# Moving the first norms and transposes of a transformer's last part between the last output tiles of its attention

## Chip, cores and metric

The kernel runs on one core of one Trainium2 chip. The metric is device time in microseconds (us) of one execution. Before the change three runs took 1278.79, 1281.23 and 1281.28 us, a median of 1281.23.

## What is computed

Input is x, 4 batches of 512 rows with 512 features, and a context of the same shape. Four parts follow one another, each adding to x through a gate:

```python
x = x + tanh(g_xattn[0]) * L0_xattn(layernorm(x), ctx)         # one quantized product
x = x + tanh(g_ffn[0])   * L0_ffn(layernorm(x), w1, w2)        # two quantized products, GELU
x = x + tanh(g_xattn[1]) * L1_xattn(layernorm(x), ctx, ctx)    # 16 heads, 4 key groups, alibi, Wo
x = x + tanh(g_ffn[1])   * L1_ffn(layernorm(x))                # 2 of 8 experts, plus a shared MLP

# the last part, on the 2048 normalized rows
logits = xn @ router_w.T                                       # softmax, best 2, weights that sum to 1
moe    = sum over the chosen experts of  c_e * ((silu(xn @ gate_e) * (xn @ up_e)) @ down_e)
shared = (silu(xn @ s_gate + b) * (xn @ s_up + b)) @ s_down + b
```

The change lies at the border between the third part (attention) and the last.

## The kernel before

**Tiles.** Rows are held in 16 tiles of 128 (`x_sb[:, t, :]`, t = 0 to 15, four to a batch). x stays on the chip throughout. Everything is float32 except where the parts quantize. A float32 product of 128 x 512 shows as two passes in the profile, a transpose as one.

**Who orders the work.** The program is written in one sequence; a list scheduler then reorders it engine by engine, each instruction being issued when its inputs and memory are free, and the one written earlier going first. Two helpers restrain it. `tc.keep_in_program_order(ins)` ties an instruction behind the one that was written just before it on the same engine, and `tc.issue_after(ins)` ties a block behind a given instruction. Attention's products all go through `product` (line 237), which ties them, so TensorE's order in attention is the order written.

**Memory.** Tiles come from pools that lie as a stack from two ends of the on-chip memory. A pool that takes the place of closed ones can be written only when the readers of those are done.

**Attention's end.** The attention loop (lines 1095 to 1100) runs scores, softmax, weighted values and output products of different head groups interleaved. Its pools `qk` (queries and keys), `npool` and `one` (lines 1014 to 1016) are on the right side, `epool` (exponentials, partial sums, weighted values, line 1059) on the left; all four are closed together when the block of line 1058 ends. Behind the loop stand the last weighted values (`weigh`), two output products, `sums` of the last head group, and then the loop of lines 1105 to 1108. That loop does for each of the last four row tiles (12 to 15): `divide` (line 409: a reciprocal on VectorE, tied; a multiplication on GpSimd, line 414) and `given` (line 460), which is four output products of `project` (line 437) and the addition to x on VectorE (line 452). The sums depend on a chain of additions on GpSimd (`add_up`, line 389).

**The last part's start.** Behind attention come the pools `dpool` and `fpool` (lines 1116, 1117). `vx` (line 1119) holds the normalized rows with a row index and a weight beside each; 16 index fills on GpSimd write its index column (line 1121). Then come the load of the shared bias `sdb`, which is asked for on SyncE's queue (line 1126), and the loads of the shared weights (`load_shared`, line 1147). `normed(b)` (line 1160) takes the statistics of a batch (`layer_norm_stats`, line 115) and gives back four steps. Each normalizes one row tile on VectorE (`layer_norm`, line 129, instruction L130), transposes it in four pieces on TensorE into PSUM (L1170) and copies it to `xnT` on ScalarE (L1173). The steps of batch 0 run by themselves (lines 1296, 1297), those of the following batches between the gate and up products of the batch before (`shared_hidden`, line 1212, products L1219). The PSUM pool `big` has three buffers, which the transposes and the gate and up products share. Behind all batches come routing, the sorting of rows by expert through `slots` in device memory, the second half of the shared MLP and 36 tiles of expert rows, whose results are added to the output by indirect DMA (L1499).

Of the kernel before, what the change touches and what calls it, by code (L numbers as in the profile page):

```python
# [10 lines left out]
F32 = mybir.dt.float32  # L11
BF16 = mybir.dt.bfloat16
I32 = mybir.dt.int32
# [7 lines left out]
P = 128  # L21
B, S, D = 4, 512, 512
NT = B * S // P
TB = S // P
DC = D // P
# [10 lines left out]
RW = D + 2  # L36
# [12 lines left out]
def flamingo_kernel(  # L49
# [29 lines left out]
    def big(name):  # L79
        return ps_big.tile([P, 2, 512], F32, tag="big", name=name)  # L80
# [34 lines left out]
    def layer_norm_stats(b, tag, add=nc.vector):  # L115

        t0 = b * TB
        mv = small.tile([P, TB, 2], F32, tag="mv", name=f"mv_{tag}_{t0}")
        for i in range(TB):
            st = small.tile([P, 6], F32, tag="st", name=f"st_{tag}_{t0 + i}")  # L120
            nc.vector.bn_stats(st, x_sb[:, t0 + i, :])
            nc.vector.bn_aggr(mv[:, i, :], st)
        ve = small.tile([P, TB], F32, tag="ve", name=f"ve_{tag}_{t0}")
        add.tensor_scalar_add(ve, mv[:, :, 1], LN_EPS)
        rstd = small.tile([P, TB], F32, tag="rstd", name=f"rstd_{tag}_{t0}")
        nc.gpsimd.tensor_tensor(rstd, ve, mhalf, ALU.pow)
        return mv, rstd

    def layer_norm(dst, t, i, mv, rstd):
        nc.vector.tensor_scalar(  # L130
            dst, x_sb[:, t, :], mv[:, i, 0:1], rstd[:, i : i + 1], ALU.subtract, ALU.mult
        )
# [261 lines left out]
    def sums(b, g):  # L394
        parts = state.pop(("sum", b, g))
        sm = acc(f"sm_{b}_{g}")
        for k, part in enumerate(parts):
            for i in range(HPG):
                product(
                    sm[32 * i : 32 * i + 32, :],  # L400
                    lhsT=ones[:, :DH],
                    rhs=part[:, i, :],
                    start=k == 0,
                    stop=k == len(parts) - 1,
                )
        state["rec", b, g] = epool.tile([P, S], F32, tag="rec", name=f"rec_{b}_{g}", bufs=2)
        nc.scalar.copy(state["rec", b, g], sm)
# [647 lines left out]
            turn_units(1, 3)  # L1055


    with attention as ph:
        epool = ph.enter_context(tc.tile_pool(name="epool", bufs=3))
        wo_sb = place(2, "wo")[:, : DC * D].rearrange("p (c n) -> p c n", c=DC)  # L1060
        nc.sync.dma_start(out=wo_sb, in_=wo.rearrange("(c p) n -> p c n", p=P))


        rt_sb = const.tile([P, DC, 32], F32, name="rt_sb")
        nc.gpsimd.memset(rt_sb, 0.0)
        nc.sync.dma_start(out=rt_sb[:, :, :E], in_=routerT.rearrange("(c p) e -> p c e", p=P))
        sgb = const.tile([P, 2, 3], F32, name="sgb")
        sub = const.tile([P, 2, 3], F32, name="sub")
        nc.sync.dma_start(out=sgb, in_=s_gate_b)
        nc.sync.dma_start(out=sub, in_=s_up_b)  # L1070

        dram = ctx.enter_context(tc.tile_pool(name="dram", bufs=1, space=bass.MemoryType.DRAM))
        slots = dram.tile([MT * P, RW], F32, name="slots")
        empty = row_tables[:, 3 * NG * S + B * P :][:, : 2 * RW].bitcast(F32)
        nc.gpsimd.memset(empty, 0.0)
        nc.gpsimd.iota(
            empty[:, D : D + 1].bitcast(I32), [[0, 1]], base=B * S, channel_multiplier=1
        )

        def clear_slots(j0, j1):  # L1080
            if j0 < j1:
                nc.sync.dma_start(
                    out=slots[j0 * P : j1 * P, :].rearrange("(j p) d -> p j d", p=P),
                    in_=empty.unsqueeze(1).to_broadcast([P, j1 - j0, RW]),
                )


        before = const.tile([P, P], BF16, name="before")
        nc.gpsimd.memset(before, 1.0)
        nc.gpsimd.affine_select(  # L1090
            before, before, [[1, P]], ALU.is_gt, 0.0, base=0, channel_multiplier=-1
        )
        ones_h = const.tile([P, P], BF16, name="ones_h")
        nc.gpsimd.memset(ones_h, 1.0)
        for n in range(2, last_n + 3):
            for u in range(TB):
                turn_units(n, u)
            if n <= last_n:
                with tc.issue_after(state["fetch"]):
                    clear_slots(min(3 * (n - 2), MT), min(3 * (n - 2) + 3, MT))  # L1100
        weigh(*state["pend"])
        o3[2]()
        o3[3]()
        sums(*groups[-1])
        for i in range(TB):
            divide(*groups[-1], i)
            for f in given(NT - TB + i):
                f()

# [1 line left out]

    dpool = ctx.enter_context(tc.tile_pool(name="dpool", bufs=1))
    fpool = ctx.enter_context(tc.tile_pool(name="fpool", bufs=2))

    vx = dpool.tile([P, NT, RW], F32, name="vx")
    for t in range(NT):  # L1120
        nc.gpsimd.iota(
            vx[:, t, D : D + 1].bitcast(I32), [[0, 1]], base=t * P, channel_multiplier=1
        )
    places = [place(k, f"w_{k}") for k in range(3)]
    sdb = dpool.tile([P, D], F32, name="sdb")
    nc.sync.dma_start(out=sdb, in_=s_down_b.partition_broadcast(P))
# [27 lines left out]

    shared_w = [load_shared(n) for n in range(2)]

    xnT = dpool.tile([P, DC, NT * P], F32, name="xnT_d")
    prob = dpool.tile([P, NT, E], F32, name="prob")

    def normed(b):  # L1160

        state["d"] = layer_norm_stats(b, "d", nc.gpsimd)

        def one_tile(i):
            t = b * TB + i
            v = vx[:, t, :D]
            layer_norm(v, t, i, *state["d"])
            tp = big(f"tpd_{t}")
            for dc in range(DC):
                nc.tensor.transpose(  # L1170
                    tp[:, 0, dc * P : (dc + 1) * P], v[:, dc * P : (dc + 1) * P], ident
                )
            nc.scalar.copy(  # L1173
                xnT[:, :, t * P : (t + 1) * P], tp[:, 0, :].rearrange("p (c q) -> p c q", q=P)
            )

        return [lambda i=i: one_tile(i) for i in range(TB)]

    def routed():

        lgT = acc("lgT")
        for dc in range(DC):
            for b in range(B):
                nc.tensor.matmul(
                    lgT[32 * b : 32 * b + 32, :],
                    lhsT=rt_sb[:, dc, :],
                    rhs=xnT[:, dc, b * S : (b + 1) * S],
                    start=dc == 0,
                    stop=dc == DC - 1,
                )  # L1190
        strips = fpool.tile([P, S], F32, tag="row", name="strips", bufs=5)
        nc.scalar.copy(strips, lgT)
        tp = acc("tpr")
        for i in range(TB):
            nc.tensor.transpose(
                tp[:, i * P : (i + 1) * P], strips[:, i * P : (i + 1) * P], ident
            )
        nc.vector.tensor_copy(
            prob.rearrange("p (b i) e -> p b i e", b=B),
            tp.rearrange("p (i b e) -> p b i e", i=TB, b=B)[:, :, :, :E],  # L1200
        )
# [10 lines left out]
    def shared_hidden(n, b, h, chunks, between=()):  # L1212
        gw, uw, _ = shared_w[n]
        between = list(between)
        for c in range(chunks):
            gu = big(f"gu_{n}_{b}_{c}")
            for m, w in enumerate((gw, uw)):
                for dc in range(DC):
                    nc.tensor.matmul(  # L1219
                        gu[:, m, :],  # L1220
                        lhsT=w[:, dc, c * P : (c + 1) * P],
                        rhs=xnT[:, dc, b * S : (b + 1) * S],
                        start=dc == 0,
                        stop=dc == DC - 1,
                    )
            gate_up(gu, n, c, h[:, c, :], f"{n}_{b}_{c}")
            while between and (c == chunks - 1 or len(between) >= TB - c):
                between.pop(0)()

    def shared_halves(b, h):  # L1230

        gw, uw, _ = shared_w[1]
        gu = big(f"gu_h_{b}")
        for m, w in enumerate((gw, uw)):
            for dc in range(DC):
                for k in range(2):
                    nc.tensor.matmul(
                        gu[64 * k : 64 * k + 64, m, :],
                        lhsT=w[:, dc, 2 * P :],
                        rhs=xnT[:, dc, (b + k) * S : (b + k + 1) * S],  # L1240
                        start=dc == 0,
                        stop=dc == DC - 1,
                    )
        gate_up(gu, 1, 2, h, f"h_{b}")
# [48 lines left out]
                nc.sync.dma_start(out=out_t[:, t, :], in_=x_sb[:, t, :])  # L1293


    for f in normed(0):
        f()
    pend = None
    for b in range(B):
        h = hidden_rows(f"hd_0_{b}")  # L1300
# [312 lines left out]
```

## Time and profile before

| what | value |
| --- | --- |
| runs | 1278.79, 1281.23, 1281.28 us; median 1281.23 |
| the profiled execution | 1278.66 us, of which 1277.0 us span from its first to its last instruction |
| busy: TensorE | 1169.5 us, 92% of the span |
| busy: VectorE, ScalarE, GpSimd | 607.1 (48%), 510.9 (40%), 410.9 us (32%) |
| mean granted TensorE clock | 0.968 of full speed |
| read from and written to device memory | 113.84 and 32.32 MB |
| last attention score product ends | 684.83 us |
| last four output tiles on TensorE | from 692.07 us |
| first gate and up product | 710.68 us |
| router products | from 805.67 us |
| expert tiles | from about 957 us on |

All starts are counted from the beginning of the span. In lines of the profile PE is TensorE, PEld its weight loads, DVE VectorE, ACT ScalarE, POOL GpSimd and SPq the DMA queue of SyncE. A line of a timeline has start, length, engine, line of the code, operation, what it writes and reads, the shape and the number of instructions merged into it; in brackets stands how long the engine was idle before it and what ended that. `oc` are attention's output products, `tpd` the transposes of the last part's first norms, `gu` its gate and up products, `sm` attention's sums, `part` the partial sums. The busy time of TensorE contains waiting within its pipeline, so it is an upper bound.

### The profile page before, as it was taken

What the parts mean: (1) busy time and instruction counts of PE and PEld (TensorE: products, weight loads), DVE (VectorE), ACT (ScalarE), POOL (GpSimd) and SP (SyncE); (2) the same over time, 40 slices, a digit from 0 to 9 for tenths busy, and PEclk for the clock granted to TensorE, in tenths of its full rate; (3) what the DMA queues carried; (4) which work ended last, traced back from release to release, by engine and by line L of the source; (5) the groups of instructions that cost most, each with busy time, mean ns of one, the idle gap of its engine ahead of it and who ended that gap; (6) DMA issues with size and microseconds to landing.
All of it is one profiled execution on the core that took longest, in us unless ns stands there. A gap on an engine that the chain in (4) does not pass through costs nothing. (4 is left out here: it accounts for less than half of the span.)

```text
span 1277.0 us, 14308 instructions
## 1 busy us (share of the span) xinstructions
PE 1169.5 (92%) x5246; PEld 531.7 (42%) x5262; DVE 607.1 (48%) x1157; ACT 510.9 (40%) x710; POOL 410.9 (32%) x409
## 2 busy tenths in 40 slices
PE   3777897899899999999999999998999999999995
PEld 1333443344233333333333444443335555555553
DVE  7699999788557666656554511321221111111110
ACT  4688898686355554544454211100001112121121
POOL 1000100111277777767776311155000111111111
PEclk8878899999899999999999999998999999999998
DMA  9230232335021211211003000066116786888782
GB/s 342 72 131 12 42 62 42 85 79 118 28 68 34 67 35 35 67 34 59 2 1 141 9 1 1 0 230 183 62 63 189 231 266 187 262 262 253 202 247 34
DMA packets 88752, 135.32 MB, mean 106 GB/s; under 512 B 52836, under 2 KB 54120, under 8 KB 84840
## 3 DMA queue, kind: packets, MB, share of 16 engines
q1 hardware_dynamic: 80936, 116.52, 28.9%
q0 software_dynamic: 7744, 17.86, 6.6%
q8 instruction: 42, 0.69, 0.2%
q14 instruction: 30, 0.25, 0.1%
HBM read 113.84 MB, written 32.32 MB: 114 GB/s over the span
## 5 line engine op out<-in xcount | busy, mean ns | idle before, releaser
L428 ACT ACTIVATE ex<-s,mbias,mk 128x1024 f32<-128x1024 f32 x128 | 147.2, 1200 | 143.3 <-PE s L239 143.3
L319 DVE TENSOR_REDUCE nmax<-s 128x2 f32<-128x1024 f32 x128 | 150.3, 1215 | 100.4 <-PE s L239 89.6
L1463 PE MATMUL gue<-w,xT 128*128 128x352 f32 x576 | 176.1, 459 | 0.0
L1499 POOL DMA_INDIRECT out_dram<-ye,row_i x36 | 55.5, 1541 | 327.5 <-ACT ye L1498 230.1
L389 POOL TENSOR_TENSOR part<-part,ex 128x1024 f32<-128x1024 f32 x62 | 144.6, 2352 | 16.5 <-PE sm L239 11.4
L1219 PE MATMUL gu<-xnT_d,w 128*128 128x512 f32 x320 | 140.4, 593 | 0.7 <-ACT xnT_d L1173 0.7
L1463 PEld LDWEIGHTS gue<-w,xT 128*128 128x128 f32 x576 | 109.2, 190 | 70.6 <-issue 16.9
L1483 DVE COPY hT<-tph_e 128x256 f32<-128x256 f32 x36 | 15.3, 425 | 255.2 <-PE tph_e L1481 255.2
L1490 PE MATMUL oe<-w,hT 128*128 128x512 f32 (+1 forms) x216 | 102.4, 609 | 3.8 <-ACT ye L1498 0.6
L1219 PEld LDWEIGHTS gu<-xnT_d,w 128*128 128x128 f32 x320 | 59.9, 190 | 73.9 <-issue 72.1
L761 PE MATMUL oa<-ctx,vTa 128*128 128x512 f32 x128 | 69.5, 694 | 18.8 <-ACT vTa L758 18.7
L1207 ACT ACTIVATE sg<-gu,sgb 128x512 f32<-128x512 f32 x20 | 13.7, 687 | 175.9 <-PE gu L1219 154.0
L389 POOL TENSOR_TENSOR part<-ex,ex 128x1024 f32<-128x1024 f32 x32 | 75.8, 2388 | 24.1 <-ACT ex L428 24.1
L1471 ACT ACTIVATE sge<-gue 128x352 f32<-128x352 f32 x36 | 16.8, 465 | 151.5 <-PE gue L1463 151.5
L239 PE MATMUL s<-row_tables 10*128 10x512 bf16 (+1 forms) x512 | 67.7, 387 | 9.3 <-DVE nmax L319 5.9
L239 PE MATMUL s<-k,qT 32*128 32x512 f32 x512 | 72.8, 610 | 0.4 <-ACT qT L287 0.4
L239 PE MATMUL s<-qT,k 32*128 32x512 f32 x512 | 71.8, 601 | 0.0
L239 PE MATMUL av<-ex,kv 128*32 128x512 f32 x512 | 70.1, 612 | 0.4 <-ACT ex L428 0.4
L239 PE MATMUL q_ps<-xnT,wq_sb 128*128 128x512 f32 (+1 forms) x156 | 69.4, 557 | 0.0
L912 PE MATMUL ob<-w2q,hqT 128*128 128x512 bf16 x248 | 58.8, 381 | 11.3 <-DVE hqT L838 10.4
L1208 DVE SCALAR_TENSOR_TENSOR hd<-gu,sub,sg 128x512 f32<-128x512 f32 x20 | 15.0, 750 | 111.7 <-ACT sg L1207 98.8
L239 PE MATMUL oc<-wo,attnT 128*128 128x512 f32 (+1 forms) x164 | 66.2, 525 | 0.0
(261 smaller groups left out, 1648.6 us busy)
## 6 DMA issues: line engine op xcount, KB each, us to landing
w<-in_e_w_dram SPq DMA_DIRECT2D x36, 1408.0 KB
w<-in_e_w_dram SPq DMA_DIRECT2D x36, 768.0 KB
slots<-row_tables SPq DMA_DIRECT2D x13, 771.0 KB
xr<-slots SPq DMA_DIRECT2D x36, 256.0 KB
stage<-in_w1T_dram SPq DMA_DIRECT2D x4, 1024.0 KB
stage<-in_w2T_dram SPq DMA_DIRECT2D x4, 1024.0 KB
k<-kv SPq DMA_DIRECT2D x64, 64.0 KB
out_dram<-x_sb SPq DMA_DIRECT2D x16, 256.0 KB
```

The lines of the kernel that those rows point to most:

```text
L239: tc.keep_in_program_order(nc.tensor.matmul(*args, **how))
L319: largest = nc.vector.tensor_reduce(nmax[:, i, 2 * j : 2 * j + 2], sc[j], AX.X, ALU.max, negate=True)
L389: nc.gpsimd.tensor_tensor(part[:, hs, :], old[:, hs, :], ex[:, hs, :], ALU.add)
L428: nc.scalar.activation(ex[:, 2 * j : 2 * j + 2, :], sc[j], AF.Exp, bias=mbias[:, b, kc : kc + 1], scale=mk[:, b, kc : kc + 1],)
L761: nc.tensor.matmul(o_ps[:, 0, :], lhsT=vT[:, dc, :], rhs=cq[:, dc, :], start=dc == 0, stop=dc == DC - 1,)
L912: nc.tensor.matmul(o_ps, lhsT=hqT[:, c, :], rhs=w2q[:, c * D : (c + 1) * D], start=c == 0, stop=c == IC - 1,)
L1219: nc.tensor.matmul(gu[:, m, :], lhsT=w[:, dc, c * P : (c + 1) * P], rhs=xnT[:, dc, b * S : (b + 1) * S], start=dc == 0, stop=dc == DC - 1,)
L1463: nc.tensor.matmul(gu[:, m, :I], lhsT=xT[:, dc, :], rhs=wt[:, dc, :], start=dc == 0, stop=dc == DC - 1,)
L1471: nc.scalar.activation(sg, gu[:, 0, :I], AF.Silu)
L1483: nc.vector.tensor_copy(hT[:, :2, :], tp[:, : 2 * P].rearrange("p (c q) -> p c q", q=P))
L1490: nc.tensor.matmul(o_ps[:, 0, :], lhsT=hT[:ni, c, :], rhs=dw[:ni, c, :], start=c == 0, stop=c == len(ICH) - 1,)
L1499: added = nc.gpsimd.indirect_dma_start(out=out, out_offset=bass.IndirectOffsetOnAxis(ap=row_i[:, j, 0:1].bitcast(I32), axis=0), in_=y, in_ ...
```

## The change

Attention's right-hand pools are closed before the last four output tiles, and `epool` gets a block of its own that stays open. A pool `rows` on the right takes `vx` and the transposed block of batch 0. `normed(0)` is called before the loop over the last four tiles, and each of its four steps runs behind the output products of one tile. The transposes of batch 0 are tied to the order written. The transposed rows become one block for each batch; those of batches 1 to 3 and the rest of `dpool` are on the right, too. The two lines that ran `normed(0)` behind attention are gone.

```diff
-    with attention as ph:
+    with ExitStack() as ph:
         epool = ph.enter_context(tc.tile_pool(name="epool", bufs=3))
...
         sums(*groups[-1])
+
+        attention.close()
+        rows = ctx.enter_context(tc.tile_pool(name="rows", bufs=1, side="right"))
+        vx = rows.tile([P, NT, RW], F32, name="vx")
+        for t in range(NT):
+            nc.gpsimd.iota(
+                vx[:, t, D : D + 1].bitcast(I32), [[0, 1]], base=t * P, channel_multiplier=1
+            )
+        xnT = [rows.tile([P, DC, S], F32, name="xnT_d_0")]
+
+        def normed(b):
+
+            state["d"] = layer_norm_stats(b, "d", nc.gpsimd)
+
+            def one_tile(i):
+                t = b * TB + i
+                v = vx[:, t, :D]
+                layer_norm(v, t, i, *state["d"])
+                tp = big(f"tpd_{t}")
+                for dc in range(DC):
+                    turned = nc.tensor.transpose(
+                        tp[:, 0, dc * P : (dc + 1) * P], v[:, dc * P : (dc + 1) * P], ident
+                    )
+                    if b == 0:
+                        tc.keep_in_program_order(turned)
+                nc.scalar.copy(
+                    xnT[b][:, :, i * P : (i + 1) * P], tp[:, 0, :].rearrange("p (c q) -> p c q", q=P)
+                )
+
+            return [lambda i=i: one_tile(i) for i in range(TB)]
+
+        first_norms = normed(0)
         for i in range(TB):
             divide(*groups[-1], i)
             for f in given(NT - TB + i):
                 f()
+            first_norms[i]()
...
-    dpool = ctx.enter_context(tc.tile_pool(name="dpool", bufs=1))
+    dpool = ctx.enter_context(tc.tile_pool(name="dpool", bufs=1, side="right"))
...
-    vx = dpool.tile([P, NT, RW], F32, name="vx")
...
-        nc.gpsimd.iota(
...
+    xnT += [dpool.tile([P, DC, S], F32, name=f"xnT_d_{b}") for b in range(1, B)]
...
-    xnT = dpool.tile([P, DC, NT * P], F32, name="xnT_d")
...
-    for f in normed(0):
-        f()
     pend = None
```

In the products that read it, `xnT[:, dc, b * S : (b + 1) * S]` becomes `xnT[b][:, dc, :]`.

More of the change, by code (lines that the diff above doesn't have):

```diff
@@ L1108, in flamingo_kernel @@
                 f()
-    dpool = ctx.enter_context(tc.tile_pool(name="dpool", bufs=1))
+            first_norms[i]()
+    dpool = ctx.enter_context(tc.tile_pool(name="dpool", bufs=1, side="right"))
     fpool = ctx.enter_context(tc.tile_pool(name="fpool", bufs=2))
-    vx = dpool.tile([P, NT, RW], F32, name="vx")
-    for t in range(NT):
-        nc.gpsimd.iota(
-            vx[:, t, D : D + 1].bitcast(I32), [[0, 1]], base=t * P, channel_multiplier=1
-        )
+    xnT += [dpool.tile([P, DC, S], F32, name=f"xnT_d_{b}") for b in range(1, B)]
     places = [place(k, f"w_{k}") for k in range(3)]
@@ L1155, in flamingo_kernel @@
     shared_w = [load_shared(n) for n in range(2)]
-    xnT = dpool.tile([P, DC, NT * P], F32, name="xnT_d")
     prob = dpool.tile([P, NT, E], F32, name="prob")
[L1160 to L1177, printed above, removed]
     def routed():
@@ L1186, in routed @@
                     lhsT=rt_sb[:, dc, :],
-                    rhs=xnT[:, dc, b * S : (b + 1) * S],
+                    rhs=xnT[b][:, dc, :],
                     start=dc == 0,
@@ L1221, in shared_hidden @@
                         lhsT=w[:, dc, c * P : (c + 1) * P],
-                        rhs=xnT[:, dc, b * S : (b + 1) * S],
+                        rhs=xnT[b][:, dc, :],
                         start=dc == 0,
@@ L1239, in shared_halves @@
                         lhsT=w[:, dc, 2 * P :],
-                        rhs=xnT[:, dc, (b + k) * S : (b + k + 1) * S],
+                        rhs=xnT[b + k][:, dc, :],
                         start=dc == 0,
```

## The prediction, made before the result was known

> **What bounds the kernel now.** I read in this order: the page's busy shares (TensorE 92%), the chain that ended last, the stage table, the waits of TensorE, and then the timeline of each engine around the edit. The chain names only 19% of the span (the row additions at the end, and the time between them) and does not reach back to the edit, so the limit there has to come from the stages. In the stage table each row gives the stretch, its length, and then busy us of TensorE, its weight loads, VectorE, ScalarE and GpSimd, the granted clock, the DMA share and GB/s.
>
> ```profile
> 692.00:706.00 14.00, 14.00 (x36) 5.95 (x32) 7.98 (x13) 0.58 (x1) 3.09 (x6) 1.00 0.34 144
> 706.00:711.00 5.00, 2.66 (x18) 1.98 (x18) 4.89 (x10) 2.52 (x5) 2.66 (x19) 1.00 0.16 56
> 711.00:861.00 150.00, 150.00 (x456) 67.21 (x454) 36.90 (x86) 19.74 (x31) 36.97 (x34) 1.00 0.13 47
> 861.00:867.00 6.00, 0.50 (x2) 0.37 (x2) 1.83 (x3) 0.69 (x1) 2.02 (x4) 0.72 0.45 156
> 867.00:945.00 78.00, 78.00 (x201) 31.40 (x200) 13.75 (x19) 4.81 (x7) 14.90 (x16) 0.98 0.32 102
> 945.00:1258.00 313.00, 309.71 (x1066) 180.42 (x1067) 44.45 (x113) 57.61 (x106) 52.40 (x34) 1.00 0.75 220
> ```
>
> TensorE is full before 706 and after 711, and half idle in between: that is where attention's last outputs end and the last part begins. After 711 it stays full but for one hole at 861 to 867 (below). So time taken out at 706 to 711 should reach the end nearly whole: everything behind hangs on products that start from there. The waits of TensorE from 706 to 950 (total, times, longest) put names on both holes.
>
> ```profile
> PE od L1255 <- DVE x_sb L1262: 5.5, 1, 5.5
> PE tpd L1170 <- DVE vx L130: 1.7, 2, 1.4
> PE gu L1219 <- ACT xnT_d L1173: 0.7, 1, 0.7
> ```
>
> The second and third belong to the edit: transposes wait for the first norms, and the first gate and up product for the copy out of PSUM. TensorE's timeline, start and length:
>
> ```profile
> 692.07 14.00 PE L239 MATMUL oc<-wo,attnT 128*128 128x512 f32 x32
> 707.46 0.63 PE L1170 MATMUL tpd<-ident,vx 128*128 128x128 f32 x4 [1.39 <-DVE vx L130]
> 708.36 1.64 PE L1170 MATMUL tpd<-ident,vx 128*128 128x128 f32 x12 [0.27 <-DVE vx L130]
> 710.68 7.13 PE L1219 MATMUL gu<-xnT_d,w 128*128 128x512 f32 x16 [0.67 <-ACT xnT_d L1173]
> ```
>
> The four output tiles are 32 passes in 13.72 us (0.429 each; two passes a product), without a gap. Then 4.89 us lie between the pass that would follow (692.07 + 13.72 = 705.79) and the first gate product (710.68), for 16 transposes of 0.107 us each (1.72 us; 717.65 to 718.08 shows four in 0.43). Some 3.2 us of that is waiting.
>
> **Why the norms start late today.** Mean, variance and 1/sigma of these four tiles are ready at 542 us, so the rows do not hold them up. vx does: it lies in the pool that takes attention's memory, and its 16 index fills on GpSimd start at 706.15, released by the last output product. The change puts vx and the first transposed block where queries and keys lay; their last reader is the score product that ends at 684.83. VectorE then stands idle for 6.63 us, up to 690.29.
>
> **What the change moves, and its sum.**
> 1. Transposes of tiles 0 to 2 go between the output products, those of tile 3 behind them. If no norm is late, the passes end at 705.79 + 3 x 0.43 = 707.08, where tile 3's transposes start. A copy starts 0.78 us after the first of its four transposes (717.65 to 718.43), takes 0.58, and the product follows 0.05 later (710.63 to 710.68): 708.49. Against 710.68 that is **2.19 us gained**. The copies of tiles 0 to 2 lie on an idle ScalarE (15.38 us idle before its first copy). If that cover were gone, each is 0.58.
> 2. Four norms (0.54 us each) move from VectorE's queue behind the last output addition to where their inputs are ready. The order in the code isn't the order of issue: the statistics written at line 1296 ran at 542. I expect all four in the idle stretch before 690.29, and next to them those of tiles 4 to 7, whose 1/sigma is ready at 637. Nothing else on VectorE waits there; but GpSimd is at work:
>
> ```profile
> 685.10 2.35 POOL L389 TENSOR_TENSOR part<-part,ex 128x1024 f32<-128x1024 f32 x1
> 687.42 0.45 POOL L414 TENSOR_TENSOR attnT<-attnT,rec 128x128 f32<-128x128 f32 x1
> 687.83 2.34 POOL L389 TENSOR_TENSOR part<-part,ex 128x1024 f32<-128x1024 f32 x1
> 690.18 1.09 PE L239 MATMUL sm<-part,ones 128*32 128x512 f32 x8
> ```
>
> The sums of the last group start at 690.18, the moment the last addition ends (690.17), with TensorE free at 690.25: slack 0.07 us. Whatever slows these additions stops TensorE. Norms beside GpSimd additions are seen once in this trace:
>
> ```profile
> 715.64 3.83 DVE L130 TENSOR_SCALAR vx<-x_sb,mv_d,rstd_d 128x512 f32<-128x512 f32 x4 [1.48 <-POOL rstd_d L126]
> 716.27 5.55 POOL L1429 TENSOR_TENSOR x_sb<-x_sb,sdb 128x512 f32<-128x512 f32 x4 [0.66 <-DVE vx L130]
> ```
>
> Four norms take 3.83 us rather than 2.16 and four additions 5.55 rather than 5.05 (1.26 each alone): two collisions at 0.25 us for GpSimd. The Trainium skill ("SBUF — State Buffer", section "SBUF: two separate sides") speaks against this move: it has VectorE in its two-port modes and GpSimd exclude each other for a whole instruction, whoever starts first. By that rule, three norms between the pieces above cost 3 x 0.54 = 1.6 us; by the row 3 x 0.25 = 0.75, less the slack, 0.7. I take **0.7 us lost**, since the row is the same instruction; the ends are 0 (norms after 690.2) and 1.6.
> 3. The 16 index fills (128 ns each; as a group 1.25 us on GpSimd) move ahead of the four divisions L414. They can start at 684.83, behind the additions already due, in the idle from 690.17 to 692.08: nothing. In front of an addition they would cost up to 1.25.
> 4. Reciprocals are tied to the VectorE instruction written before them: today the output addition L452 of the tile before (reciprocal at 696.48, right behind L452 at 695.81), in the change a norm. The divisions come earlier, but TensorE does not wait for them today, so nothing is gained: 0 to 0.1.
> 5. The norms of tiles 4 to 7 being early, some of their transposes can stand in TensorE's wait for the last copy (708.49 - 707.51 = 0.98 us), as two output passes written later stand in the same wait at 733.13 today. Each tile put there is 0.43 us less later. I take one tile: **0.4 gained**; ends 0 and 0.86.
> 6. One transposed block per batch instead of one for all, and the last part's pool at the other end of memory: no instruction more. The pool still overlaps attention's last buffers, so the bias load (706.15 now) stays where it is, and no load on SyncE's queue moves past another. The shared weights are asked for at 684.02, and DMA moves nothing in 711 to 735, so they have landed. Cost: nothing. Were the bias load put ahead of them and held till 706.15, the first half of their 4.4 MB (moved in some 16 us today: 204 GB/s to 692, then 144 GB/s averaged to 706) would land near 714.5, 6 us late.
>
> Sum: 2.19 - 0.7 + 0.4 = 1.9 us. The profiled execution took 1278.66 us (span 1277.0, 1.66 around it), so its like would take 1276.8. The median of the three runs shown is 1281.23, 2.6 above it, so I forecast 1281.2 - 1.9 = **1279.3**. The runs of one kernel lie 2.5 us apart; 0.2% (2.56 us) is about what a measurement of this kernel can tell from no change.
>
> **Rivals.**
> - *Clean, gain above 2.56.* Norms miss the additions and two tiles fill the wait: 2.19 + 0.86 = 3.05, time 1278.2. For it: VectorE's order is free in 684 to 690. Against: norms become ready just there.
> - *Nothing left.* The norms hold the additions by whole instructions (1.6), or fills or transposes of tile 4 stand before the sums and wait for a held norm (another 0.4 to 1): gain 0 to 0.6, time 1281.0. For it: the slack of 0.07. Against: collisions at 0.25.
> - *Slower: norms behind the output additions.* The new transposes hold all of TensorE, because they stand in its queue between the output tiles. If VectorE issues norm i behind L452 of the same round, as written, TensorE waits at each tile for L452 (starts 0.31 us after the tile's last slot, as 695.81 against 695.50), 0.67 to the norm's start (706.11 to 706.78) and 0.68 to the transpose (706.78 to 707.46): 1.66 us. Four rounds: gate products at 692.07 + 4 x (3.43 + 1.66 + 0.43) + 0.98 = 715.1, 4.4 us later than today: 1285.7. It decides above 2.19 / 4 = 0.55 us a round. Against: 6.63 us of idle VectorE with all inputs ready.
> - *The hole at 861* (5.5 us: ScalarE starts sg_h at 864.45 though its product ended at 855.79, while the DMA share is 1.0). Its cause isn't in the trace; with another count of instructions on an engine it may close (1274) or grow (1284).
>
> **Chances.** Forecast (gain 1 to 2.5) 0.46, clean 0.20, nothing left 0.16, slower by the wait 0.10, the hole 0.08 (half each way). Faster by over 0.2%: clean 0.20, hole 0.04, edge of the forecast 0.07: 0.31. Slower: 0.10 + 0.04 = 0.14. Within: 0.55. The range leaves out the whole of the slower wait and most of the hole's two ends: 1275.8 to 1283.0; the cases near no change and the spread of the runs make its width. The forecast's own range is 1278.7 to 1280.2.
>
> **What would show it.** Right: vx norms at 685 to 692; four transposes between output tiles with no wait for L130; first gate product some 2 us nearer to the start of the output tiles (16.4 us after it, now 18.6); the four L413 close together. Step 2: sums later than 690.2 with the wait put to POOL part, or not. Wrong: waits of transposes for L130, index fills among L389, the bias load issued ahead of the shared weights, or a changed hole at 861.

## The result, and the profile after

The change made the kernel slower, by 0.24%. Over 11 runs each, the kernel before has a median of 1280.80 us and the changed kernel 1283.18 us; the ratio is 1.0024 with a 95% interval of 1.0016 to 1.0031, some 3 us (2.0 to 4.0). The forecast was a gain of 1.9 us, and the time lies just above the range's end. The profiled execution of the changed kernel took 1281.25 us (span 1279.5), against 1278.66 (span 1277.0) before.

The stage table after, with the same columns as in the prediction (start and end, length, busy us of TensorE, its weight loads, VectorE, ScalarE and GpSimd, granted clock, DMA share, GB/s):

```profile
692.00:706.00 14.00, 11.17 (x36) 4.99 (x31) 10.86 (x19) 1.76 (x3) 3.23 (x7) 1.00 0.35 146
706.00:711.00 5.00, 5.00 (x16) 2.28 (x15) 1.63 (x3) 0.59 (x1) 0.00 (x0) 1.00 0.01 3
711.00:861.00 150.00, 149.32 (x458) 67.45 (x457) 34.92 (x82) 20.70 (x32) 37.00 (x36) 1.00 0.12 45
861.00:867.00 6.00, 1.69 (x4) 0.38 (x2) 0.31 (x1) 0.69 (x1) 2.18 (x4) 1.00 0.67 235
867.00:945.00 78.00, 76.85 (x194) 31.30 (x195) 14.51 (x20) 4.81 (x7) 15.62 (x16) 0.96 0.32 102
```

The half-idle stretch at 706 to 711 is full now, as foreseen. But the stretch ahead of it, in which TensorE was full before (14.00), has lost 2.83 us. The waits of TensorE from 640 to 712 (total, times, longest) name what came in:

```profile
PE oc L239 <- POOL attnT L414: 2.0, 1, 2.0
PE oc L239 <- DVE x_sb L452: 0.9, 1, 0.9
```

Neither was there before. Both belong to the output products of tile 12, the first of the four: the lower one is for their PSUM buffer, which the output addition L452 of tile 11 has to empty (L77: two buffers, and the sums take the one between), the upper one for the division L414 of the last group, which the last two of the tile's eight passes need. The timeline of TensorE shows where:

```profile
693.57 2.84 PE L239 MATMUL oc<-wo,attnT 128*128 128x512 f32 x6 [0.86 <-DVE x_sb L452]
698.38 1.12 PE L239 MATMUL oc<-wo,attnT 128*128 128x512 f32 x2 [1.97 <-POOL attnT L414]
699.34 0.60 PE L1125 MATMUL tpd<-ident,vx 128*128 128x128 f32 x4
...
710.96 0.60 PE L1125 MATMUL tpd<-ident,vx 128*128 128x128 f32 x4
712.23 7.13 PE L1228 MATMUL gu<-xnT_d,w 128*128 128x512 f32 x16 [0.68 <-ACT xnT_d L1130]
```

The part that was to bring the gain works: four transposes stand between output tiles without a wait for a norm, and the last group of them is followed 1.27 us later by the first gate product. But tile 12 is late twice, so that this product starts at 712.23 us instead of 710.68.

**Where the lateness comes from.** VectorE's timeline before the change around the same place, then after:

```profile
690.29 0.75 DVE L452 SCALAR_TENSOR_TENSOR x_sb<-oc,tg,x_sb 128x512 f32<-128x512 f32 x1 [6.63 <-PE oc L239]
...
692.86 0.95 DVE L413 RECIPROCAL rec<-rec 128x128 f32<-128x128 f32 x1 [0.87 <-ACT rec L407]
```

```profile
684.89 7.96 DVE L130 TENSOR_SCALAR vx<-x_sb,mv_d,rstd_d 128x512 f32<-128x512 f32 x8 [1.27 <-PE s L239]
692.77 0.74 DVE L452 SCALAR_TENSOR_TENSOR x_sb<-oc,tg,x_sb 128x512 f32<-128x512 f32 x1
693.54 0.69 DVE L121 BATCH_NORM_STATS2 st_d<-x_sb 128x6 f32<-128x512 f32 x1
694.27 0.18 DVE L122 BATCH_NORM_AGGREGATE mv_d<-st_d 128x2 f32<-128x6 f32 x1
695.93 1.00 DVE L130 TENSOR_SCALAR vx<-x_sb,mv_d,rstd_d 128x512 f32<-128x512 f32 x2 [1.47 <-POOL rstd_d L126]
696.85 2.57 DVE L413 RECIPROCAL rec<-rec 128x128 f32<-128x128 f32 x3
```

The 6.63 us of idle time ahead of L452 are gone: eight norms fill them, and they do not fit. Eight at 0.54 us are 4.3 us; here they take 7.96, so L452 of tile 11 starts at 692.77 instead of 690.29. That is the first wait. The eight are far from even (shortest, median and longest in ns):

```profile
L130 DVE TENSOR_SCALAR vx<-x_sb,mv_d,rstd_d x8: 529/544/2589, 684.9 to 692.3; 128x512 f32<-128x512 f32 x8
```

The statistics of tile 11 hang on L452 and follow late; 1/sigma of tiles 8 to 11 comes from GpSimd (L126, 694.85 to 695.89), and two more norms that waited for it stand ahead of the first reciprocal of the last group: 696.85 instead of 692.86, 3.99 us late. What the reciprocal itself needs, ScalarE's copy of the sums, is there at 693.40:

```profile
692.81 0.59 ACT L407 COPY rec<-sm 128x512 f32<-128x512 f32 x1 [3.88 <-PE sm L239]
```

GpSimd's division follows at 697.87. That is the second wait.

GpSimd's timeline after, in the same stretch:

```profile
685.06 2.60 POOL L389 TENSOR_TENSOR part<-part,ex 128x1024 f32<-128x1024 f32 x1
687.61 0.64 POOL L414 TENSOR_TENSOR attnT<-attnT,rec 128x128 f32<-128x128 f32 x1
688.21 2.53 POOL L389 TENSOR_TENSOR part<-part,ex 128x1024 f32<-128x1024 f32 x1
690.70 1.30 POOL L1110 IOTA vx<- 128x1 int32 x16
694.85 1.04 POOL L126 TENSOR_TENSOR rstd_d<-ve_d,mhalf 128x4 f32<-128x4 f32 x1
697.87 0.45 POOL L414 TENSOR_TENSOR attnT<-attnT,rec 128x128 f32<-128x128 f32 x1 [1.98 <-DVE rec L413]
```

The three pieces that took 2.35, 0.45 and 2.34 us take 2.60, 0.64 and 2.53: three collisions of 0.25, 0.19 and 0.19, and the last addition ends at 690.74 instead of 690.17. This is the loss that the prediction had in its sum.

To compare kernels whose traces begin a little apart, I count TensorE's times from one instruction ahead of the edit: the start of the weighted values of the third key block of the last group (684.76 before, 684.71 after). From there to the first gate product it is 25.92 us before and 27.52 after: 1.60 us late. The account closes: tile 12 starts 8.86 us after the mark instead of 7.31, which is 1.55 late (0.86 the wait for L452, the other 0.69 behind the late additions); its last two passes start at 698.38, where an unbroken row would have them at 693.57 + 6 x 0.429 = 696.14, which is 2.24 (1.97 of waiting, and 0.27 for the end of a pass that no other overlaps); together 3.79 lost, less the 2.19 gained, is 1.60. This stays so up to the product at 850. The 5.5 us wait for L1271 (L1262 before) is there in both, but the twelve passes behind it differ. Before, then after:

```profile
866.63 7.33 PE L1255 MATMUL od<-w,hd 128*128 128x512 f32 x12 [5.50 <-DVE x_sb L1262]
```

```profile
868.15 8.34 PE L1264 MATMUL od<-w,hd 128*128 128x512 f32 x12 [5.46 <-DVE x_sb L1271]
```

Without a wait ahead of them, twelve such passes show as 5.42 us (12 x 0.429, and the end of the last one), so 1.9 us are lost there before and 2.9 after; the end is 2.64 us late by the traces. What is lost is TensorE's clock. The stretch 868 to 874, before, then after:

```profile
868.00:874.00 6.00, 6.00 (x12) 2.53 (x11) 0.75 (x1) 0.00 (x0) 4.48 (x5) 0.79 0.54 210
868.00:874.00 6.00, 5.85 (x7) 2.52 (x8) 1.01 (x3) 0.00 (x0) 4.48 (x6) 0.50 0.51 196
```

In both traces the granted clock is 0.50 for 6.8 us: from 863.7 to 870.5 before, from 867.2 to 874.1 after. The passes go on at 866.63 and 868.15, so 3.9 and 5.9 us of half clock lie behind the wait, and half of that is the loss of 1.9 and 2.9.

### The profile page after: what moved, and what is told of

Same layout as the page of the kernel before. It is cut to its first block, busy times and chain, and to the rows that moved or that the text cites. A ratio compares the mean times of both kernels' runs of the same rounds, so it can differ in the third digit from the quotient of the medians.

```text
span 1279.5 us, 14304 instructions
## 1 busy us (share of the span) xinstructions
PE 1167.2 (91%) x5246; PEld 530.9 (41%) x5262; DVE 610.4 (48%) x1157; ACT 511.1 (40%) x710; POOL 411.5 (32%) x409
## 5 line engine op out<-in xcount | busy, mean ns | idle before, releaser
L389 POOL TENSOR_TENSOR part<-part,ex 128x1024 f32<-128x1024 f32 x62 | 145.1, 2360 | 16.4 <-PE sm L239 11.4
L389 POOL TENSOR_TENSOR part<-ex,ex 128x1024 f32<-128x1024 f32 x32 | 75.8, 2393 | 24.3 <-ACT ex L428 24.2
L761 PE MATMUL oa<-ctx,vTa 128*128 128x512 f32 x128 | 64.8, 653 | 19.9 <-ACT vTa L758 19.8
L912 PE MATMUL ob<-w2q,hqT 128*128 128x512 bf16 x248 | 61.6, 395 | 12.5 <-DVE hqT L838 10.4
```

The lines of the kernel that those rows point to most:

```text
L389: nc.gpsimd.tensor_tensor(part[:, hs, :], old[:, hs, :], ex[:, hs, :], ALU.add)
L761: nc.tensor.matmul(o_ps[:, 0, :], lhsT=vT[:, dc, :], rhs=cq[:, dc, :], start=dc == 0, stop=dc == DC - 1,)
L912: nc.tensor.matmul(o_ps, lhsT=hqT[:, c, :], rhs=w2q[:, c * D : (c + 1) * D], start=c == 0, stop=c == IC - 1,)
```

## The experiments

The first question was which of the change's parts does the harm. Theory A said: the norms stand in VectorE's queue ahead of L452 and the reciprocals. Theory B said: the new transposes, tied to their place, hold TensorE. The first gate product, counted as above, is the measure that depends least on what happens elsewhere. All edits are made on the changed kernel. Two groups of kernels ran on two chips, each beside the kernel before on the same chip (medians 1272.3 and 1280.3 us); only ratios and the counted difference are compared across the two, and on which chip the first measurement ran is not on record. The first four kernels told of below are the first group (with "last sums on TensorE" as the fourth); in their traces there is no wait for L1271 at 861.

| kernel | first gate product against before, us | ratio to before, 95% interval |
|---|---|---|
| the change (first measurement) | +1.60 | 1.0024 (1.0016 to 1.0031) |
| later norms behind L452 | -1.80 | 0.9987 (0.9981 to 0.9994) |
| all new norms behind the reciprocals | -2.17 | 0.9981 (0.9973 to 0.9988) |
| the memory alone | +2.12 | 1.0021 (1.0009 to 1.0033) |
| last sums on TensorE | 0.00 | 0.9998 (0.9990 to 1.0006) |
| transposes behind the loop | -2.02 | 0.9982 (0.9975 to 0.9989) |
| only the third batch's norms behind | -0.18 | 0.9997 (0.9989 to 1.0006) |
| two more tiles in the wait | -2.14 (router -3.04) | 0.9979 (0.9971 to 0.9987) |
| the change again | +1.83 | 1.0024 (1.0016 to 1.0031) |

**Later norms behind L452.** Norms of tiles 4 to 15 are tied behind the output addition that is written last, those of tiles 0 to 3 stay free.

```diff
-            nc.vector.scalar_tensor_tensor(
+            state["added"] = nc.vector.scalar_tensor_tensor(
                 x_sb[:, t, :], o_ps, tg[:, 1:2], x_sb[:, t, :], ALU.mult, ALU.add
-            )
+            ).ins
...
-                layer_norm(v, t, i, *state["d"])
+                with tc.issue_after(state["added"]) if b > 0 else nullcontext():
+                    layer_norm(v, t, i, *state["d"])
```

> The change, with the norms of tiles 4 to 15 tied behind the last output addition on VectorE; only the four norms of batch 0 stay in the stretch before 690. Theory A (VectorE's queue: six later norms in front of the output addition of tile 11 and of the first reciprocal make TensorE wait 0.9 and 2.0 us): the four norms end near 691.0, output addition of tile 11 near 691.0, first reciprocal near 693.4, no wait of the output products for L452 or L414; sums still 0.5 us late; first gate product near 709.1, 1.6 us before the old kernel's 710.7; ratio to the kernel before 0.9988. Theory B (the transposes tied between the output tiles hold TensorE): waits stay, gate product near 712. Theory C (the loss is the additions on GpSimd, slowed by the norms): the same four collisions, gate product near 712.

The first gate product came 1.80 us earlier than before the change, where the change itself had it 1.60 later. VectorE's timeline:

```profile
685.51 6.37 DVE L130 TENSOR_SCALAR vx<-x_sb,mv_d,rstd_d 128x512 f32<-128x512 f32 x4 [1.27 <-PE s L239]
691.80 0.73 DVE L452 SCALAR_TENSOR_TENSOR x_sb<-oc,tg,x_sb 128x512 f32<-128x512 f32 x1
...
693.82 3.39 DVE L413 RECIPROCAL rec<-rec 128x128 f32<-128x128 f32 x4 [0.34 <-ACT rec L407]
```

Four norms still take 6.37 us beside GpSimd's additions (the shortest 0.54, the longest 2.81), and L452 comes right behind them. It is in time for TensorE, and so are the reciprocals. The tied transposes are all still there: Theory B falls. So does the expectation's Theory C, that GpSimd's slowed additions are the whole loss: they meet norms here as well. The 0.37 us by which this is short of the next kernel are the late sums.

**All new norms behind the reciprocals.** The four norms of batch 0 are tied as well, each behind the reciprocal of its round.

```diff
-        tc.keep_in_program_order(nc.vector.reciprocal(r, r))
+        state["recip"] = tc.keep_in_program_order(nc.vector.reciprocal(r, r)).ins
...
-                layer_norm(v, t, i, *state["d"])
+                with tc.issue_after(state["added" if b > 0 else "recip"]):
+                    layer_norm(v, t, i, *state["d"])
```

> As the last, and the norms of batch 0 too are tied, each behind the reciprocal of its round, so that no norm runs beside the last additions of GpSimd. Theory A: sums start at 690.2 as in the kernel before, output products at 692.1 without a wait, first gate product near 708.5, a gain of 2.2 us; ratio 0.9983. The first multiplication on GpSimd may collide with the first norm, up to 0.3 us. Theory B: each transpose waits for a norm that stands behind a reciprocal, gate product near 711 or later.

Measured: 2.17 us earlier, where the prediction's first step had 2.19. No norm meets one of GpSimd's additions any more (three of the four divisions L414 still meet one, 0.60 us instead of 0.45), L452 is back behind 6.63 us of idle time, and the norms lie between reciprocals:

```profile
691.27 0.75 DVE L452 SCALAR_TENSOR_TENSOR x_sb<-oc,tg,x_sb 128x512 f32<-128x512 f32 x1 [6.63 <-PE oc L239]
...
693.84 0.95 DVE L413 RECIPROCAL rec<-rec 128x128 f32<-128x128 f32 x1 [0.88 <-ACT rec L407]
694.71 0.45 DVE L130 TENSOR_SCALAR vx<-x_sb,mv_d,rstd_d 128x512 f32<-128x512 f32 x1
```

**The memory alone.** vx and the first block stay in the memory of queries and keys, but the four steps of the first norms stand behind the loop, and the transposes are not tied.

```diff
-                    turned = nc.tensor.transpose(
+                    nc.tensor.transpose(
...
-                    if b == 0:
-                        tc.keep_in_program_order(turned)
...
-        first_norms = normed(0)
...
-            first_norms[i]()
+        for f in normed(0):
+            f()
```

> Only the memory of the change: normalized rows and the first transposed block where queries and keys were; norms and transposes of batch 0 are written behind the output tiles as before, and nothing of them is tied. Theory A: the scheduler takes the freed memory and puts the same norms into the same stretch of VectorE's queue, so the waits for L452 and L414 are there without any transpose between the tiles; output products stop for 3 us, first gate product near 712.2 as in the change. Theory B: no transpose stands between the tiles, so the gate product comes near 709.

It is as late as the change, 2.12 us, with the same two waits of TensorE:

```profile
PE oc L239 <- POOL attnT L414: 2.1, 1, 2.1
PE oc L239 <- DVE x_sb L452: 1.3, 1, 1.3
```

So neither the place at which the norms are written nor the fixed order of the transposes does the harm. It comes with the memory: once vx is free (at 686.03 in this trace), the norms are ready, and they are issued then, wherever they are written. The reciprocals are tied behind L452 here, as before the change, and two norms of the third batch stand ahead of the first one all the same:

```profile
697.29 1.00 DVE L130 TENSOR_SCALAR vx<-x_sb,mv_d,rstd_d 128x512 f32<-128x512 f32 x2 [1.47 <-POOL rstd_d L126]
698.20 0.95 DVE L413 RECIPROCAL rec<-rec 128x128 f32<-128x128 f32 x1
```

**Last sums on TensorE.** Built on the change itself, with the transposes between the tiles (so its reference is +1.60, or +1.83 when measured again). The two additions L389 of the last group that fall into the norms' time are left out on GpSimd; TensorE sums these parts with its ones instead. This takes away what the norms collide with.

```diff
-        if kc == TB - 1 and (b, g) == groups[-1]:
+        if kc >= TB - 2 and (b, g) == groups[-1]:
...
+            if kc < TB - 1:
+                return
```

> The change, but the last head group's third block of exponentials isn't added on GpSimd; TensorE sums three parts instead of two (8 passes more, some 0.95 us). GpSimd has no addition beside the norms then. If the exclusion between VectorE and GpSimd is what makes the eight norms last 7.96 us: they take 8 x 0.54 = 4.3 us and end near 689.3, the output addition of tile 11 is on time at 690.3, the first reciprocal near 694.6, and the first gate product near 709.8. If the norms are slow for another reason, they stay at 8 us and the gate product at 712 to 713.

```profile
686.71 4.10 DVE L130 TENSOR_SCALAR vx<-x_sb,mv_d,rstd_d 128x512 f32<-128x512 f32 x8 [1.27 <-PE s L239]
692.06 0.75 DVE L454 SCALAR_TENSOR_TENSOR x_sb<-oc,tg,x_sb 128x512 f32<-128x512 f32 x1 [1.26 <-PE oc L239]
...
695.23 1.91 DVE L130 TENSOR_SCALAR vx<-x_sb,mv_d,rstd_d 128x512 f32<-128x512 f32 x4 [1.47 <-POOL rstd_d L126]
697.06 2.57 DVE L415 RECIPROCAL rec<-rec 128x128 f32<-128x128 f32 x3
```

The collision is confirmed: the same eight norms take 4.10 us instead of 7.96, and the output addition (L454 in this kernel) has 1.26 us to spare. The total is a miss: 0.00 instead of -0.9. All four norms of tiles 8 to 11 stand ahead of the reciprocal now, and TensorE waits 1.1 us for the division; the eight more passes of the sums put tile 12 another 0.83 us back (8.14 us after the mark, 7.31 before the change). The collision and the norms ahead of the reciprocal are two causes, and this experiment removes only one of them.

**Only the third batch's norms behind.** The other half: norms of tiles 8 to 15 are tied behind the last reciprocal written, those of tiles 0 to 7 stay free.

```diff
-                layer_norm(v, t, i, *state["d"])
+                with tc.issue_after(state["recip"]) if b > 1 else nullcontext():
+                    layer_norm(v, t, i, *state["d"])
```

> The change, with only the norms of batches 2 and 3 tied behind the last reciprocal; the eight norms of batches 0 and 1 stay in front of the output addition of tile 11. It parts the two waits of the change. Theory A: the wait of the output products for L452 (0.9 us, a PSUM buffer that the late addition holds) stays, the wait for the multiplication L414 (2.0 us) goes, since the reciprocals no longer stand behind norms that wait for the statistics of tile 11. First gate product 0.4 us before the old kernel's instead of 1.6 behind; ratio 0.9997. If the eight norms alone delay the reciprocals, the 2.0 us stay.

Measured: -0.18 (0.4 earlier was expected), with one wait left, that for L452, which is 1.3 us here and not the 0.9 of the first trace:

```profile
PE oc L239 <- DVE x_sb L452: 1.3, 1, 1.3
```

```profile
686.22 8.18 DVE L130 TENSOR_SCALAR vx<-x_sb,mv_d,rstd_d 128x512 f32<-128x512 f32 x8 [1.27 <-PE s L239]
694.33 0.74 DVE L452 SCALAR_TENSOR_TENSOR x_sb<-oc,tg,x_sb 128x512 f32<-128x512 f32 x1
...
695.93 3.35 DVE L413 RECIPROCAL rec<-rec 128x128 f32<-128x128 f32 x4
```

Against the change run beside it (+1.83) this is 2.01 us, the whole of its 2.0 us wait for L414. What the eight norms of batches 0 and 1 cost is then the rest: -0.18 against -2.17, 1.99 us.

**Transposes behind the loop.** As "all new norms behind the reciprocals", but the sixteen transposes stand behind the last output tile, in their fixed order. It prices the place of the transposes by itself.

```diff
-            first_norms[i]()
+            first_norms[i] = first_norms[i]()
+        for f in first_norms:
+            f()
...
+                if b == 0:
+                    return lambda: turn(t, i, b, v)
```

> As the kernel with every norm behind its round's reciprocal (no norm beside the last additions), but the transposes and copies of batch 0 stand behind the four output tiles again. It takes the place of the transposes apart from the time of the norms. All norms are done when the output products end, so TensorE goes on at once with 16 transposes; the four copies of 0.58 us follow one another: first gate product 0.78 + 4 x 0.58 + 0.05 = 3.15 us behind the first transpose, against 2.70 with the transposes in between. So 1.7 us before the old kernel counted from the same score product, 0.45 less than the 2.17 with the transposes in between; ratio 0.9987. If the place of the transposes matters more than the time of the norms, the gain falls to below 1 us.

```profile
693.15 14.00 PE L239 MATMUL oc<-wo,attnT 128*128 128x512 f32 x32
706.99 1.94 PE L1131 MATMUL tpd<-ident,vx 128*128 128x128 f32 x16
709.73 7.13 PE L1236 MATMUL gu<-xnT_d,w 128*128 128x512 f32 x16 [0.81 <-ACT xnT_d L1136]
```

A miss in size: it gains 2.02 us, only 0.15 less than with the transposes spread, not 0.45. From the first transpose to the gate product it is 2.74 us. Nearly all of the gain comes from norms that are early, which needs the memory; that the transposes are spread between the output tiles is worth 0.15 us.

**Two more tiles in the wait.** As "all new norms behind the reciprocals", and the norms of batch 1 are tied there too; the transposes of tiles 4 and 5 are written ahead of the gate products, so that they lie in the wait for the last copy.

```diff
-                with tc.issue_after(state["added" if b > 0 else "recip"]):
+                with tc.issue_after(state["added" if b > 1 else "recip"]):
...
+    second = normed(1)
+    for f in second[:2]:
+        f()
```

The two steps left, `second[2:]`, are what the first shared half then takes along.

> As the kernel with every norm behind its round's reciprocal, and two tiles of batch 1 written ahead of the first gate product, their norms behind the last reciprocal, so that their transposes stand in the 0.98 us in which TensorE waits for the last copy. First gate product at the same place (2.17 us before the old kernel's), then 0.86 us less up to batch 1: 3.0 us in all, ratio 0.9976. If a third buffer of PSUM holds up the first gate product, the gain stays at 2.2 or falls below.

```profile
704.34 3.60 PE L239 MATMUL oc<-wo,attnT 128*128 128x512 f32 x8
707.78 1.47 PE L1126 MATMUL tpd<-ident,vx 128*128 128x128 f32 x12
709.09 20.84 PE L1229 MATMUL gu<-xnT_d,w 128*128 128x512 f32 x48
```

Twelve transposes lie between the last output pass and the gate product, which starts without a wait and 2.14 us earlier than before. The 0.86 us that two tiles cost later are gone, so the router stands 3.04 us earlier. The ratio is the lowest of all, 0.9979 (0.9971 to 0.9987), and clear of both the kernel before and the change; from "all new norms behind the reciprocals" (0.9973 to 0.9988) the times can't tell it apart.

**The change again**, unedited, on the chip of the last group.

> The change itself on the chip of these runs, where the wait of 5.5 us near 861 is absent in the four kernels run so far. First gate product 1.6 us later than the old kernel's, counted from the same score product, and the rest of the span unchanged: ratio 1.0013. If the change also costs something behind that, 1.002 or more.

```profile
PE oc L239 <- POOL attnT L414: 2.0, 1, 2.0
PE oc L239 <- DVE x_sb L452: 1.3, 1, 1.3
PE od L1264 <- DVE x_sb L1271: 5.3, 1, 5.3
```

Its trace is 1.83 us late at the first gate product and 1.49 at the end; the ratio is again 1.0024. Two expectations missed: the chip of these runs is not that of the first four kernels, and the wait at 861 is there; and the ratio is not the 1.0013 of a loss at the gate product alone. Here the wait at 861 does not add to the loss. The medians are 2.3 us apart (1282.61 and 1280.34).

## Why the prediction was wrong

**Step 1 was right.** The way from the last output pass to the gate product is shortened by 2.19 us in the forecast, by 2.17 where nothing else disturbs it. Its reason was partly off: the place of the transposes brings 0.15 of it, the early norms the rest.

**Step 2 failed**, at one sentence: "Nothing else on VectorE waits there; but GpSimd is at work". The prediction saw the collision and priced it for one of the two engines only, though its own row had VectorE's side too (four norms in 3.83 us rather than 2.16). GpSimd lost 0.57 us by the end of its last addition (0.62 counted from the mark), close to the 0.7 forecast. VectorE lost 7.96 - 4.10 = 3.86 us, for which the sum had nothing, and this had a price, because L452 of tile 11 stands behind the norms in VectorE's own queue. The sums and the output tiles share two PSUM buffers, so a late L452 of tile 11 is a wait of TensorE at tile 12. The idle time of 6.63 us was counted as cover without asking when the instruction behind it has to run: from 684.89, where their memory is free, eight norms at 0.54 would have ended 1.1 us ahead of 690.29; at their price beside GpSimd they pushed L452 back by 2.5.

The Trainium skill ("SBUF — State Buffer", section "SBUF: two separate sides"), by which VectorE's two-port modes and GpSimd keep each other out for whole instructions, was weighed against the row and put aside, with only GpSimd's side in view. For GpSimd the smaller figure was right, but the rule does not speak against it: the 1.6 us that the prediction put down to it charged each addition a whole norm, where the one that comes second has only the rest of the first to wait for. In the change that rest was 0.32 to 0.37 us at the three meetings (the first norm ends at 685.44, the addition starts at 685.06), and GpSimd lost 0.19 to 0.25. On VectorE's side the traces agree with the rule: in the change, where the median norm takes 0.54 us, one that meets the addition of 2.60 us lasts 2.59. (No trace names the mode in which a norm runs.) A rule of exclusion has two sides, and the costly side was that of the engine whose instruction is short.

**Step 4 failed.** It had the divisions come earlier, at a gain of 0 to 0.1. The first of them came later, at 697.87 instead of 693.89, and TensorE's wait of 2.0 us for it cost 2.24, the larger of the two losses. The step looked at the ties alone. The last three reciprocals are tied behind a norm in the change, as it says; the first is tied behind the statistics of batch 0, which are written just ahead of it and were done at 542. What held it was no tie but VectorE's order: two norms of tiles 8 and 9, which no step of the prediction counts, stood ahead of it and waited for their 1/sigma until 695.9, while its own input was there at 693.40. "The memory alone", where the ties are those of the kernel before, has the same two norms in front and a wait of 2.1 us; "only the third batch's norms behind" takes the wait away.

**Step 5 failed** in a small way: in the change no transposes of batch 1 stand in the wait for the last copy; the gate product waits 0.68 us for it, as before. The 0.4 us were not gained. "Two more tiles in the wait" shows that they are to be had if the code says so.

**Steps 3 and 6 were right.** The index fills run in one stretch behind the last addition (690.70), and the bias load is issued at 711.20, behind the shared weights.

**The sum.** Forecast: 2.19 - 0.7 + 0.4 = 1.9 us gained. Shown: 2.19 gained, 0.69 lost at the sums, 0.86 at L452, 2.24 at L414: 1.60 lost. The first two terms were right, the third did not come, and the two waits were not in the sum. The rival that ended slower put the norms behind L452 of their round. It was the other way about, L452 behind the norms, and at one tile instead of four; the time came out slower than the forecast, but not by that mechanism nor at its 1285.7.

**What stays open.** The edit's own loss is 1.6 to 1.8 us in two traces. The ratio's interval begins at 2.0 us and the medians are 2.3 to 2.4 apart. So at least 0.2 us of the slowdown, and by the middle of the interval about 1.3, are not located. The half clock behind the wait at 861 costs a further 1.0 us in the first trace and nothing more than before in the second (7.18 us for the twelve passes). A faster version has the long form as well (8.39 in "transposes behind the loop"), so it can't be laid to the change; but a term that moves by 1.2 us between two traces of one kernel could hold what is missing, and one trace of each measurement can't show whether it does. Nor do the traces show what causes that wait, or how far into it the clock falls (2.6 us before, 4.6 in the first trace of the change, 2.1 in the second): the wait is absent in all four traces of the first group, among them that of "the memory alone", and present in the other traces told of here.

## What to carry to other kernels

Memory that comes free earlier makes work ready earlier, and the scheduler may then put all of it, not only the part that was meant, ahead of an instruction that the limiting engine waits for. Cost such work in its own engine's queue: what stands behind it, when that has to run, and how long the work takes beside what runs then, not alone. If it isn't urgent, tie it behind the instruction that is: here, tying the norms behind the reciprocals and output additions turned 1.60 us late into 2.17 us early.

## What the runs showed of the hardware

A norm of 128x512 on VectorE, 0.5 us alone (eight in 4.10), is held for about as long as the GpSimd addition it meets (2.57 to 2.81 us for one that meets an addition of 2.34 to 2.60): four took 6.37 us beside additions, eight 7.96 to 8.19. GpSimd's addition of 128x1024 lost 0.2 to 0.25 us in the same meeting (2.35 to 2.60). So the same contention was worth 3.9 us on one engine and 0.6 on the other.

TensorE lost more behind the wait at 861 than the wait's own 5.3 to 5.5 us. In each of the six traces told of here that have it, the granted clock falls to 0.50 within the wait and stays there for about 6.8 us, and the passes that fall into the rest of that time take 0.85 us instead of 0.43: twelve passes took 7.18 to 8.39 us, and 5.42 where the clock was full. In the four traces without the wait the clock is 1.00 throughout this stretch.
